# Layer 2 of a two-layer image network: LayerNorm with tokens on partitions, the depthwise convolution inside the input projection, and a written plan for the order of the work

## The chip, the cores and the metric

The kernel runs on one core of a Trainium2 chip, in float32. The metric is the device time of one execution in microseconds. Engines are named as in the profile: PE multiplies matrices and transposes, DVE is the vector engine, ACT computes functions of one argument with a scale and a bias for each partition, POOL is the fourth one, SP issues DMAs.

## The reference, cut to what matters

Four images of 192 channels and 128 x 128 pixels go through two residual layers. The first (spectral, FFT and fractional FFT) is not touched. The second is a selective state-space layer over the 16,384 pixels of an image taken as a sequence of tokens, on the group-normalised image:

```python
x = x + layer1(group_norm(x))          # layer1, for tokens l and channels c:
seq = (seq - mu) * rsqrt(var + 1e-5) * ln_g + ln_b        # over the 192 channels of a token
xs, z = split(in_proj_w @ seq)                            # 384 and 384
u  = silu(depthwise_conv(xs, 4 taps, causal) + conv_b)
dt, B, C = split(x_proj_w @ u)                            # 12, 16, 16
dt = softplus(dt_proj_w @ dt + dt_proj_b)
for each token l:                                         # state h: 384 x 16
    h = h * exp(dt[l] * A) + (dt[l] * u[l]) * B[l]
    y[l] = sum over states of h * C[l]
out = out_proj_w @ ((y + u * D) * silu(z))
```

## The kernel before

`layer0` runs first and leaves its result in DRAM (`xmid`) and the group norm's mean and scale for each channel in `st2`. `layer1` then takes the four images one after the other in chunks of T = 512 tokens: 32 chunks an image, 128 in all. The 384 inner channels are three tiles j of 128 partitions, the 16 states are eight pairs sg. A chunk is therefore 24 steps (`NGR`), step k being tile k // 8 and pair k % 8, and the kernel 3072 steps. `order` lists them, and the loop over `order` writes the instructions of every engine in one hand-made order (the scheduler is off).

**A step.** DVE runs two scans of 512 tokens, one for each state of the pair, into `h` (L903); each takes a decay exp(dt A) from ACT (L833) and an input dt u B. POOL multiplies both states by C (L916, `hc`). Three steps later (LAG) PE adds the pair into `py` with eight transposing passes (L929, `sums`). The last value of each scan goes to the next chunk by a small DMA (L914).

**Where the input dt u B comes from** depends on the pair. V pairs: DVE multiplies the PSUM copy `dp` of dt u (L816, ACT) by B (L853, `product`), two states ahead, into one of three PSUM tiles `op`. O pairs (BY_POOL, 7 a chunk): POOL makes both states at once (L861, `inputs`), and the decay goes to an `op` tile instead. P pairs (BY_PE, pairs 3 and 6 of each tile, 6 a chunk): dt u is turned to tokens by PE (L867, `turned`), ACT scales it by B there, four blocks a state (L877, `scale_pair`), and PE turns it back into an `op` tile (L889, `turned_back`). That leaves 11 V pairs.

**After the eight pairs of a tile** come `add_skip` (L943, u D on PE), `evacuate` (L938, ACT copies `py`), `turn` (L953, PE turns it to channels) and `gate` (L958, DVE multiplies by silu(z)). After three tiles, `finish` projects out in two halves (L967, PE) and DVE adds the residual (L973).

**The front** makes dt, u, z, B and C for a chunk two ahead. It is the generator `front`, advanced by one `yield` a step; a plain yield goes on at the start of the next step, MID between the two scans of it, LATE after them. With channels on partitions it normalises (L643), sums over channels by PE (L650), subtracts (L653, DVE), squares (L658), sums again (L666), takes root and reciprocal (L673, L676), and brings the result for each token back to all channels by a transpose and four small matmuls (L678, L682, L686) for DVE's second pass (L691). Then come the input projection (L697), the copy of its x half with three columns of the chunk before (L706, L710, L711), the convolution as four diagonal matmuls a tile (L716), silu (L724, L728), the projection to dt, B, C (L762, L765) with a trip through DRAM for B and C (L767), dt (L776, contraction over 12 rows; L781), dt u (L785, POOL), B by tokens (L791, L794) and the other two z tiles.

B and C are read back for a pair of states at a time, broadcast to 128 partitions, 1 MB a DMA (L807, `load_bc`), into eight buffers, five steps ahead.

**What sets the order.** Each engine runs its instructions in the order written; SP's queue holds load_bc, the carries, the loads and stores. An instruction that waits for a buffer holds all behind it. PSUM has eight banks: three that everything of `psum()` takes in turn (`ps1`), one for `dp`, three for `op`, one for `py`.

Of the kernel before, what the change touches and what calls it, by code (L numbers as in the profile page):

```python
# [10 lines left out]
F32 = mybir.dt.float32  # L11
# [3 lines left out]
ALU = mybir.AluOpType  # L15
# [518 lines left out]

def layer1(tc, xmid, out, st2, w, n_tok=S * S):
# [5 lines left out]
    LAG, FRONT, BCL = 3, 14, 5  # L541
    AHEAD = 4

    BY_POOL = ((1, 4, 7), (1, 7), (1, 7))
    BY_PE = 3, 6
    MID, LATE = "mid", "late"

    TURNED = {0: 0, 9: 1, 15: 2, 19: 2}
    SCALED = {0: (0, 3), 3: (0, 6), 9: (1, 3), 11: (1, 6), 16: (2, 3), 20: (2, 6)}
    with ExitStack() as ctx:  # L550
# [5 lines left out]
        xp = pool("l1x", 3)  # L556
# [3 lines left out]
        bcp = pool("l1b", NS // G)  # L560
        scp = pool("l1s", 4)
        op = pool("l1o", 1)
        ps1 = pool("l1p", 3, space=PSUM)
        psd = pool("l1q", 1, space=PSUM)
        psa = pool("l1a", 3, space=PSUM)
        psy = pool("l1y", 1, space=PSUM)

        def const(name):
            src = w[name]
            t = cp.tile(list(src.shape), F32, name="c_" + name)  # L570
            nc.sync.dma_start(out=t, in_=src)
            return t

        wiT, ln_g, ln_b, xpT, dtT, dtb = (const(k) for k in ("wiT", "ln_g", "ln_b", "xpT", "dtT", "dtb"))
        cw, cb, dp, woT, A = (const(k) for k in ("cw", "cb", "dp", "woT", "A_log"))

        ident = cp.tile([128, 128], F32, name="ident")
        make_identity(nc, ident)
        ones = cp.tile([128, CH], F32, name="ones")
        nc.vector.memset(ones, 1.0)  # L580
        sel = cp.tile([4, 4, CH], F32, name="sel")
        nc.vector.tensor_copy(sel, _bc(ident[0:4, 0:4], 2, CH))
# [7 lines left out]
        )  # L590


        bxz = cp.tile([128, 2 * NJ], F32, name="bxz")
        ps = ps1.tile([128, 512], F32, name="ps")
        for m in range(2 * NJ):
            for t in range(2):
                nc.tensor.matmul(
                    ps[:, m : m + 1], wiT[:, t, m * 128 : (m + 1) * 128], ln_b[:, t : t + 1],
                    start=t == 0, stop=t == 1,
                )  # L600
        nc.vector.tensor_copy(bxz, ps[:, 0 : 2 * NJ])
        for t in range(2):
            nc.vector.tensor_scalar(wiT[:, t, :], wiT[:, t, :], ln_g[:, t : t + 1], None, ALU.mult)

# [6 lines left out]
        dcw = cp.tile([128, NJ, 4, 128], F32, name="dcw")  # L611
        for j in range(NJ):
            for k in range(4):
                nc.vector.tensor_scalar(dcw[:, j, k, :], ident, cw[:, j, k : k + 1], None, ALU.mult)

        halo = cp.tile([128, NJ, 3], F32, name="halo")
        last = {}

        def psum():
            return ps1.tile([128, 512], F32, name="ps")  # L620

# [4 lines left out]

        def load_x(i):
            b, ch = divmod(i, NCHUNK)
            xm = xp.tile([CH, 2, T], F32, name="xm")
            nc.sync.dma_start(  # L630
                out=xm, in_=xmid[b][:, ch * T : (ch + 1) * T].rearrange("(t p) f -> p t f", p=CH)
            )
            got[i]["xm"] = xm

        def front(i):

            b, ch = divmod(i, NCHUNK)
            g = got[i]
            xm = g["xm"]
            yield MID  # L640
            s = lp.tile([CH, 2, T], F32, name="s", bufs=2)
            for t in range(2):
                nc.scalar.activation(  # L643
                    s[:, t, :], xm[:, t, :], AF.Identity,
                    bias=nmr[:, b, t : t + 1], scale=st2[:, b, t, 1:2],
                )
            yield
            mu = psum()
            for t in range(2):
                nc.tensor.matmul(mu[0:CH], ones[0:CH, :], s[:, t, :], start=t == 0, stop=t == 1)  # L650
            yield
            yield MID
            nc.vector.scalar_tensor_tensor(  # L653
                s, _bc(mu[0:CH], 1, 2), -1.0 / C, s, ALU.mult, ALU.add
            )
            yield
            sq = lp.tile([128, NJ, T + 3], F32, name="xs")[0:CH, 0:2, 0:T]
            nc.scalar.activation(sq, s, AF.Square)  # L658
            yield


            yield LATE
            var = psum()
            for q in range(4):
                for t in range(2):
                    nc.tensor.matmul(  # L666
                        var[:, q : q + 1], sq[:, t, q * 128 : (q + 1) * 128], ones[0:CH, 0:1],
                        start=t == 0, stop=t == 1,
                    )
            yield  # L670
            yield LATE
            rs = tp.tile([128, 4], F32, name="rs")
            nc.scalar.activation(rs, var[:, 0:4], AF.Sqrt, bias=eps, scale=1.0 / C)  # L673
            yield
            yield LATE
            nc.vector.reciprocal(rs, rs)  # L676
            rt = psum()
            nc.tensor.transpose(rt[0:4, 0:128], rs, ident)  # L678
            yield
            yield MID  # L680
            rows = tp.tile([4, 128], F32, name="rows")
            nc.scalar.copy(rows, rt[0:4, 0:128])  # L682
            yield LATE
            rb = psum()
            for q in range(4):
                nc.tensor.matmul(  # L686
                    rb[0:CH, q * 128 : (q + 1) * 128], sel[:, q, :], rows, start=True, stop=True
                )
            yield
            yield MID  # L690
            nc.vector.tensor_tensor(s, s, _bc(rb[0:CH], 1, 2), ALU.mult)  # L691
            yield

            def in_proj(m):
                pp = psum()
                for t in range(2):
                    nc.tensor.matmul(  # L697
                        pp, wiT[:, t, m * 128 : (m + 1) * 128], s[:, t, :], start=t == 0, stop=t == 1
                    )
                return pp  # L700

            xs = lp.tile([128, NJ, T + 3], F32, name="xs")
            if ch == 0:
                nc.gpsimd.memset(xs[:, :, 0:3], 0.0)
            else:
                nc.scalar.copy(xs[:, :, 0:3], halo)  # L706
            for j in range(NJ):
                pp = in_proj(j)
                yield
                nc.scalar.activation(xs[:, j, 3:], pp, AF.Identity, bias=bxz[:, j : j + 1])  # L710
            nc.scalar.copy(halo, xs[:, :, T : T + 3])  # L711
            yield LATE

            def conv(j, pc, half):
                for k in (2 * half, 2 * half + 1):
                    nc.tensor.matmul(  # L716
                        pc, dcw[:, j, k, :], xs[:, j, k : k + T], start=k == 0, stop=k == 3
                    )

            u, zs = g["u"], g["zs"] = {}, {}  # L720

            def silu_u(j, pc):
                u[j] = jp.tile([128, T], F32, name="u")
# [506 lines left out]
```

## Time and profile before

| | us |
|---|---|
| median of three runs | 11368.98 |
| lowest and highest of them | 11358.7, 11369.3 |
| profiled execution, span | 11364.2 |
| first scan of layer1 (L903) | 1426.8 |
| last scan of layer1 ends | 11347.4 |
| a chunk, from 77.5 = (11347.4 - 1426.8) / 128 | 77.5 |

The profile is of one execution; its span lies 4.8 us under the median of the runs. A line of groups has the line in the code, engine, operation, output <- inputs, partitions x elements, how many, then busy time in us and the mean of one in ns, then the idle time of the engine just before such instructions and what ended it. "PEld" is PE's weight load, which overlaps its matmuls. A matmul of float32 counts as two instructions. In the table of windows, a number in brackets is a count, and the granted clock of PE is 1.00 at full speed. "bc" and "ps" are names that several tiles share.

### The profile page before, as it was taken

What the parts mean: (1) busy time and instruction counts of PE and PEld (TensorE: products, weight loads), DVE (VectorE), ACT (ScalarE), POOL (GpSimd) and SP (SyncE); (2) the same over time, 40 slices, a digit from 0 to 9 for tenths busy, and PEclk for the clock granted to TensorE, in tenths of its full rate; (3) what the DMA queues carried; (4) which work ended last, traced back from release to release, by engine and by line L of the source; (5) the groups of instructions that cost most, each with busy time, mean ns of one, the idle gap of its engine ahead of it and who ended that gap; (6) DMA issues with size and microseconds to landing.
All of it is one profiled execution on the core that took longest, in us unless ns stands there. A gap on an engine that the chain in (4) does not pass through costs nothing.

```text
span 11364.2 us, 163771 instructions
## 1 busy us (share of the span) xinstructions
PE 10431.7 (92%) x54154; PEld 6995.9 (62%) x54154; DVE 10480.6 (92%) x11073; ACT 9340.5 (82%) x17503; POOL 9811.8 (86%) x4470
## 2 busy tenths in 40 slices
PE   4777799999999999999999999999999999999998
PEld 2444366666666666666666666666666666666666
DVE  5666599999999999999999999999999999999999
ACT  2332189989989989999989989989989999899897
POOL 0000099999999999999999999999999999999999
PEclk8888699999999999999999999999999999999998
DMA  8786644344344344344344344344344344344343
GB/s 233 195 219 170 199 123 129 108 126 129 107 126 129 107 126 129 106 127 129 105 128 129 105 128 129 104 128 129 104 128 129 104 129 129 103 129 128 104 130 99
DMA packets 1339287, 1481.93 MB, mean 130 GB/s; under 512 B 903281, under 2 KB 954214, under 8 KB 1337926
## 3 DMA queue, kind: packets, MB, share of 16 engines
q1 hardware_dynamic: 1317958, 1408.54, 42.2%
q0 software_dynamic: 13312, 50.34, 1.4%
q10 hardware_dynamic: 7168, 12.59, 0.3%
q8 instruction: 429, 7.03, 0.2%
q14 instruction: 420, 3.44, 0.1%
HBM read 1312.63 MB, written 155.32 MB: 129 GB/s over the span
## 4 chain that ended last, share of the span: by engine, by line
ACT 28%; DVE 27%; PE 25%; issue 8%; POOL 3%; DMA 1%; DVEq 0%; POOLq 0%; SPq 0%; ACTq 0%
DVE h L903 18%; ACT da L833 8%; DVE op L853 6%; PE py L929 6%; ACT dbT L877 6%; PE ps L697 4%; PE ps L716 4%; PE ps L967 4%; ACT L833 3%; PE op L889 2%; POOL db L861 2%; ACT op L833 1%; ACT L724 1%; ACT dt L781 1%; PE ps L686 1%
## 5 line engine op out<-in xcount | busy, mean ns | idle before, releaser
L916 POOL TENSOR_TENSOR hc<-h,bc 128x1024 f32<-128x1024 f32 x3072 | 7203.0, 2381 | 217.6 <-PE ps L953 145.8
L903 DVE TENSOR_TENSOR_SCAN h<-da,carry,op 128x512 f32<-128x512 f32 x4216 | 5198.7, 1261 | 22.6 <-ACT da L833 6.1
L929 PEld LDWEIGHTS py<-ident,hc 128*128 128x128 f32 x24576 | 3002.6, 149 | 855.2 <-issue 698.4
L929 PE MATMUL py<-ident,hc 128*128 128x128 f32 x24576 | 3406.0, 286 | 32.6 <-ACT yt L938 19.1
L833 ACT ACTIVATE da<-dt,c_A_log 128x512 f32<-128x512 f32 x4352 | 3003.7, 727 | 181.9 <-DVE h L903 161.6
L903 DVE TENSOR_TENSOR_SCAN h<-op,carry,db 128x512 f32<-128x512 f32 x1736 | 2200.7, 1268 | 124.2 <-POOL db L861 119.6
L861 POOL TENSOR_TENSOR db<-dtu,bc 128x1024 f32<-128x1024 f32 x896 | 2152.9, 2403 | 4.5 <-DMA bc<-dbc 4.5
L853 DVE TENSOR_TENSOR op<-dp,bc 128x512 f32<-128x512 f32 x2816 | 1886.0, 670 | 11.2 <-ACT dp L816 11.2
L833 ACT ACTIVATE op<-dt,c_A_log 128x512 f32<-128x512 f32 x1792 | 1227.0, 685 | 674.1 <-DVE h L903 671.0
L877 ACT ACTIVATE dbT<-ps,bT 128x128 f32<-128x128 f32 x6144 | 1666.6, 383 | 0.0
L697 PE MATMUL ps<-s,c_wiT 96*128 96x512 f32 x3072 | 1529.3, 622 | 5.2 <-ACT xs L710 3.6
L716 PE MATMUL ps<-xs,dcw 128*128 128x512 f32 x3072 | 1426.6, 593 | 1.4 <-ACT u L724 1.4
L889 PE MATMUL op<-ident,dbT 128*128 128x128 f32 x6144 | 1075.3, 295 | 102.1 <-DVE h L903 71.7
L889 PEld LDWEIGHTS op<-ident,dbT 128*128 128x128 f32 x6144 | 779.8, 151 | 397.2 <-ACT dbT L877 204.8
L697 PEld LDWEIGHTS ps<-s,c_wiT 96*128 96x128 f32 x3072 | 559.2, 199 | 473.7 <-issue 463.6
L833 ACT ACT_TABLE_LOAD x635 | 814.7, 1283 | 11.2
L716 PEld LDWEIGHTS ps<-xs,dcw 128*128 128x128 f32 x3072 | 533.9, 190 | 434.9 <-issue 433.3
L967 PE MATMUL ps<-yg,c_woT 128*96 128x512 f32 x1536 | 710.5, 598 | 70.3 <-DVE xm L973 70.2
L776 PE MATMUL ps<-xd,c_dtT 12*128 12x512 f32 x768 | 512.6, 756 | 162.2 <-DVE s L653 94.8
L495 POOL DMA_DIRECT2D xmid<-xt x64 | 41.7, 652 | 567.7 <-DVE xt L491 523.0
L967 PEld LDWEIGHTS ps<-yg,c_woT 128*96 128x96 f32 x1536 | 239.9, 163 | 436.9 <-issue 321.6
L785 POOL TENSOR_TENSOR dtu<-dt,u 128x512 f32<-128x512 f32 x384 | 479.3, 1284 | 33.8 <-ACT dt L781 33.8
(172 smaller groups left out, 10196.2 us busy)
## 6 DMA issues: line engine op xcount, KB each, us to landing
bc<-dbc SPq DMA_DIRECT2D x1024, 1024.0 KB, 5.7
xt<-in_x SPq DMA_DIRECT2D x176, 768.0 KB, 8.1
xmid<-xt POOLq DMA_DIRECT2D x64, 768.0 KB, 5.6
xm<-xmid SPq DMA_DIRECT2D x128, 384.0 KB, 3.5
carry<-h SPq DMA_DIRECT2D x3072, 1.0 KB, 1.9
out<-xm SPq DMA_DIRECT2D x128, 384.0 KB, 3.3
d<-x ACTq DMA_DIRECT2D x64, 192.0 KB, 6.6
df<-v SPq DMA_DIRECT2D x16, 512.0 KB, 5.4
```

The source lines that it names most:

```text
L697: nc.tensor.matmul(pp, wiT[:, t, m * 128 : (m + 1) * 128], s[:, t, :], start=t == 0, stop=t == 1)
L716: nc.tensor.matmul(pc, dcw[:, j, k, :], xs[:, j, k : k + T], start=k == 0, stop=k == 3)
L776: nc.tensor.matmul(d[j], dtT[rows, :], xd[rows, :], start=True, stop=True)
L833: nc.scalar.activation(da, got[n]["dt"][j], AF.Exp, scale=A[:, j, st : st + 1])
L853: nc.vector.tensor_tensor(dbs[s], g["dp"], g["bc", k % NG][:, 0, q, :], ALU.mult)
L861: nc.gpsimd.tensor_tensor(db, _bc(g["dtu"][j], 1, G), g["bc", sg][:, 0], ALU.mult)
L877: nc.scalar.activation(t[:, blk, :], g["tu", j][:, blk, :], AF.Identity, scale=g["bT"][:, blk, st : st + 1],)
L889: nc.tensor.transpose(db[:, blk * 128 : (blk + 1) * 128], t[:, blk, :], ident)
L903: nc.vector.tensor_tensor_scan(h[:, q, :], das.pop(s), dbs.pop(s) if db is None else db[:, q, :], 0.0 if ch == 0 else g["before"][:, j, st ...
L916: nc.gpsimd.tensor_tensor(hc, h, g["bc", sg][:, 1], ALU.mult)
L929: nc.tensor.matmul(py[:, blk, :], hc[:, q, blk * 128 : (blk + 1) * 128], ident, start=first, stop=sg == NG - 1 and q == G - 1 and blk == T ...
L967: nc.tensor.matmul(po[0:CH], woT[:, j, t * CH : (t + 1) * CH], g["yg", j], start=j == 0, stop=j == NJ - 1,)
```

## The change

It rewrites `layer1`; `layer0` stays. In the words of the code:

- LayerNorm. `to_tokens` multiplies the loaded x by a diagonal matrix `gd` of the group norm's scales, with a row of its shifts under a row of ones, so that tokens come out on partitions, two blocks of 128 tokens a bank. `moments` takes bn_stats and bn_aggr over the 192 channels on DVE, `rstd` is Ln and Exp on ACT, `shift` a small DVE instruction, `normed` four activations; `to_channels` turns the result back, and `channels` applies ln_g and ln_b on ACT and keeps three columns of the chunk before in `s`.
- The convolution is applied in the input projection. The weights `wc` are products of taps and projection, made once at the start. A tile takes six matmuls of 128 rows: four taps of the first 128 channels, and two that hold two taps of the other 64 channels each, for which a DMA copies `s[0:64]` to `s[64:128]` shifted by two columns.
- A third P pair in each tile: KINDS gives the kind of each pair, now 9 P, 6 O and 9 V. `dbT` has four buffers instead of two.
- PSUM: five banks in one list, taken by `psum` in the order of use and given back by `done`, and the three of `op` as before.
- B and C are loaded by DMAs of their own, 512 KB each; B of pair 3, which is P in all tiles, is not loaded.
- The order: PLAN says for each piece of a chunk's work the step, counted from the chunk's first, and the place in the step: S at its start, A after `turned_back` and `sums`, M between the two scans, L at its end. `log_exp` loads the table with ln and exp after each group of silu or softplus.

Cut to its core:

```diff
+KINDS = ("VOPPVVPO", "VOVPOVPP", "VOVPVPPO")
+PLAN = (
+    (-36, "A", "load_x"), (-34, "L", "to_tokens", 0), (-32, "S", "moments", 0),
+    (-32, "A", "to_tokens", 1), (-31, "S", "moments", 1), (-31, "A", "rstd"), (-30, "S", "shift"),
+    (-30, "M", "normed", 0), (-30, "M", "normed", 1), (-29, "S", "to_channels", 0),
+    (-29, "A", "channels", 0), (-28, "M", "to_channels", 1), (-28, "M", "channels", 1),
+    (-27, "S", "conv", 0, 0), (-27, "L", "conv", 1, 0), (-26, "L", "conv", 1, 1),
+    (-25, "M", "conv", 0, 1), (-24, "M", "conv", 1, 2), (-22, "L", "conv", 2, 0),
+    (-21, "M", "conv", 0, 2), (-21, "L", "silu", (0, 1), ()), (-17, "S", "conv", 2, 1),
+    (-16, "A", "conv", 2, 2), (-15, "L", "proj_z", 0), (-15, "L", "silu", (2,), (0,)),
+    (-13, "M", "proj_x"), (-11, "S", "xd_out"), (-11, "M", "proj_dt"), (-10, "M", "softplus"),
+    (-9, "M", "turn_b"), (-8, "A", "b_out"), (-7, "A", "dt_u", 0), (-7, "A", "dt_u", 1),
+    (-3, "L", "turned", 0), (-3, "L", "scale", 0, 2), (-2, "S", "dtu_copy", 0),
+    (1, "S", "dt_u", 2), (1, "A", "scale", 0, 3), (2, "S", "scale", 0, 6),
+    (4, "M", "dtu_copy", 1), (6, "S", "turned", 1), (6, "A", "scale", 1, 3),
+    (10, "S", "scale", 1, 6), (10, "A", "scale", 1, 7), (10, "M", "evacuate", 0),
+    (10, "M", "proj_z", 2), (11, "A", "proj_z", 1), (11, "M", "silu", (), (1, 2)),
+    (11, "L", "turn", 0), (12, "L", "dtu_copy", 2), (13, "M", "gate", 0), (16, "L", "turned", 2),
+    (17, "S", "scale", 2, 3), (17, "L", "scale", 2, 5), (19, "S", "scale", 2, 6),
+    (19, "M", "evacuate", 1), (21, "A", "turn", 1), (22, "S", "gate", 1),
+    (26, "L", "evacuate", 2), (29, "A", "turn", 2), (30, "A", "gate", 2),
+    (31, "A", "project_out", 0), (32, "L", "add_x", 0), (34, "S", "project_out", 1),
+    (35, "M", "add_x", 1),
+)
...
+        banks = list(range(5))
+        def psum(g, *key):
+            bank = banks.pop(0)
+            g[key] = ps1.tile([128, 512], F32, name=f"ps{bank}"), bank
+        def done(g, *key):
+            banks.append(g.pop(key)[1])
...
+            for blk in (2 * half, 2 * half + 1):
                 for t in range(2):
                     nc.tensor.matmul(
-                        var[:, q : q + 1], sq[:, t, q * 128 : (q + 1) * 128], ones[0:CH, 0:1],
+                        row(g, blk)[:, t * CH : (t + 1) * CH],
+                        g["xm"][:, t, blk * 128 : (blk + 1) * 128], gd[:, i // NCHUNK, t, :],
+                        start=True, stop=True,
+                    )
...
+            for blk in range(2):
+                nc.vector.bn_stats(st[:, blk, :], row(g, 2 * half + blk))
+            for blk in range(2):
+                nc.vector.bn_aggr(g["mv"][:, 2 * half + blk, :], st[:, blk, :])
...
+            nc.scalar.activation(rs, g["mv"][:, :, 1], AF.Ln, bias=eps)
+            nc.scalar.activation(rs, rs, AF.Exp, scale=-0.5)
...
+            for k in (2 * part, 2 * part + 1):
+                rhs = s[:, 0, k : k + T] if k < 4 else s[:, 1, 3 - 2 * (k - 4) :][:, 0:T]
+                nc.tensor.matmul(g["c", j][0], wc[:, j, k, :], rhs, start=k == 0, stop=k == 5)
...
+            if part == 1:
+                nc.sync.dma_start(out=s[64:128, 1, 1 : T + 3], in_=s[0:64, 1, 0 : T + 2])
...
+            for j in us:
+                t = g["u", j] = jp.tile([128, T], F32, name="u", bufs=5)
+                nc.scalar.activation(t, g["c", j][0], AF.Silu, bias=cb[:, j : j + 1])
+                done(g, "c", j)
+            for j in zs:
+                t = g["zs", j] = jp.tile([128, T], F32, name="zs", bufs=5)
+                nc.scalar.activation(t, g["z", j][0], AF.Silu)
+                done(g, "z", j)
+            log_exp()
...
             for pos, (n, k) in enumerate(order):
                 j, sg = divmod(k, NG)
+                act(pos, "S")
+                turned_back(G * (pos + 1))
                 if pos >= LAG and sg != LAG:
                     sums(*order[pos - LAG])
+                act(pos, "A")
                 if pos + 2 < len(order):
                     inputs(*order[pos + 2])
+                scans(pos, n, k, lambda: act(pos, "M"))
+                act(pos, "L")
                 if pos >= LAG and sg == LAG:
                     sums(*order[pos - LAG])
                     add_skip(n, j)
```

In a chunk's steps, with three chunks in work at a time, PE then meets in one step what PLAN gives for this chunk and for those one and two ahead: at step 10 project_out 1 of the chunk before and z2 of its own, at step 13 gate 0 and d of the next (-11), and so on.

## The prediction

> **What bounds the kernel now.** I read the page's first part, then the stretch from 5700 to 7700 us as windows and as groups, then single rows of the timeline, and last the waits.
>
> ```profile
> span 11364.2 us, 163771 instructions
> PE 10431.7 (92%) x54154; PEld 6995.9 (62%) x54154; DVE 10480.6 (92%) x11073; ACT 9340.5 (82%) x17503; POOL 9811.8 (86%) x4470
> ```
>
> This mixes layer 0, in which POOL does next to nothing, with 10,000 us of chunks. In a steady stretch it is closer:
>
> ```profile
> 6055.10:6061.90 6.80, 6.80 (x20) 3.92 (x19) 6.80 (x8) 6.75 (x14) 6.80 (x4) 0.50 0.04 0
> 5986.00:5989.40 3.40, 3.02 (x28) 2.81 (x28) 3.40 (x5) 3.38 (x7) 3.40 (x3) 1.00 0.12 26
> 5700.00:7700.00 2000.00, 1908.89 (x10255) 1304.06 (x10253) 1939.94 (x2015) 1810.82 (x3431) 1957.89 (x880) 0.95 0.40 119
> ```
>
> The columns after the length are PE, PEld, DVE, ACT, POOL, granted clock, DMA share, GB/s.
>
> ```profile
> L916 POOL TENSOR_TENSOR hc<-h,bc 128x1024 f32<-128x1024 f32 x620 | 1452.0, 2373 | 42.1 <-PE ps L953 29.9 <-DVE h L903 11.9
> L861 POOL TENSOR_TENSOR db<-dtu,bc 128x1024 f32<-128x1024 f32 x181 | 433.7, 2396 | 0.0
> L877 ACT ACTIVATE dbT<-ps,bT 128x128 f32<-128x128 f32 x1240 | 336.4, 383 | 0.0
> L833 ACT ACT_TABLE_LOAD x129 | 165.5, 1283 | 2.3
> L653 DVE SCALAR_TENSOR_TENSOR s<-ps,s 96x1024 f32<-96x1024 f32 x26 | 31.0, 1193 | 0.0
> L691 DVE TENSOR_TENSOR s<-s,ps 96x1024 f32<-96x1024 f32 x25 | 30.4, 1217 | 28.0 <-PE ps L686 28.0
> ```
>
> 620 hc at 24 a chunk are 25.83 chunks in 2000 us: **77.4 us a chunk**. In it POOL is busy 1957.89/25.83 = 75.8 us, DVE 75.1, PE 73.9, ACT 70.1. No engine has 8 us to spare, so the pace comes from two full engines that wait for each other, and through short queues also for PE. POOL's own idle is 1.6 us a chunk, most of it hc waiting for L953's turn on PE; DVE's 2.3 is half L691's wait for PE.
>
> A row's mean is longer than what an instruction costs in a row of its kind, since the next starts before the last ends. Start to start comes from the timeline:
>
> ```profile
> 6000.35 0.67 DVE L853 TENSOR_TENSOR op<-dp,bc 128x512 f32<-128x512 f32 x1
> 6000.93 1.27 DVE L903 TENSOR_TENSOR_SCAN h<-op,carry,db 128x512 f32<-128x512 f32 x1
> 6001.08 1.04 PE L929 MATMUL py<-ident,hc 128*128 128x128 f32 x8
> 6001.95 1.88 PE L697 MATMUL ps<-s,c_wiT 96*128 96x512 f32 x4
> 6002.71 2.44 DVE L903 TENSOR_TENSOR_SCAN h<-da,carry,op 128x512 f32<-128x512 f32 x2
> 6003.67 1.04 PE L929 MATMUL py<-ident,hc 128*128 128x128 f32 x8
> 6004.23 7.01 POOL L916 TENSOR_TENSOR hc<-h,bc 128x1024 f32<-128x1024 f32 x3
> 6007.03 2.16 ACT L877 ACTIVATE dbT<-ps,bT 128x128 f32<-128x128 f32 x8
> ```
>
> and, a chunk earlier, PE alone:
>
> ```profile
> 5978.96 1.12 PE L776 MATMUL ps<-xd,c_dtT 12*128 12x512 f32 x2 [0.59 <-ACT dbT L877]
> 5980.01 1.97 PE L929 MATMUL py<-ident,hc 128*128 128x128 f32 x8
> ```
>
> So a product takes 0.58 us (0.93 less 0.35), a scan 2.44 - 1.26 = 1.18, eight 128-column passes 0.87 (0.109 each), four 512-column passes 1.72 (0.43 each; a float32 matmul is two passes), hc (7.01 - 2.37)/2 = 2.32, a dbT (2.16 - 0.38)/7 = 0.25, a pass of d (L776) 1.05/2 = 0.53. At 5980.01 eight passes take 1.97 where they took 1.04: PE is at half clock there, as in the window from 6055.1, behind another d.
>
> **What the Trainium skill says.** "TensorE: Matmul & The Clock Gate", "Part 1: The HAM clock gate": an activity window of about 3.4 us decides between full and half clock. The trace agrees: stretches at 0.50 are 3.4 or 6.8 us long and follow d, whose operands have 12 rows. Its Part 4 says that transposes don't count as activity; the window from 5986, nearly all transposes, is at 1.00, which speaks against it, if weakly. The same page, "Architectural detail": PE pulls only weight loads ahead, ACT and DVE are strictly first in, first out. So a matmul that waits for its bank holds everything behind it; L776's waits in the middle of d above are such. "ScalarE: Activation LUTs", "Table sets": one set holds exp and ln, so the new Ln + Exp needs no load beside the decays' exp; no row of before shows it. No page read for this prices bn_stats.
>
> **The change, part by part**, per chunk, against 77.4 us.
>
> *POOL*: O pairs 7 to 6, one db less: 75.8 - 2.34 = 73.4.
>
> *DVE*: V pairs 11 to 9, four products less, -2.33. L653, L691 and the reciprocal go, -2.34. Two moments (four bn_stats of 192 elements and four bn_aggr) and the shift come. Layer 0's bn_stats of 512 takes 0.68; 192 of it between 0.25 and 0.4, a tiny instruction 0.15 to 0.19: bounds 1.6 to 2.4 with the shift, I take 1.95. Sum 75.1 - 4.67 + 1.95 = 72.4.
>
> *ACT*: P pairs 6 to 9 are 24 dbT, +6.1. Gone: two s, Square, Sqrt, rows, three xs and a halo copy, 1.6 + 1.1 + 0.3 + 0.25 + 2.15 + 0.2 = 5.6 by row means, and two of ten table loads, 2.6. New: Ln and Exp 0.5, four normed of 192 columns (bounds 0.3, 0.45) 1.4, two channels 1.3. Sum 70.1 + 1.1 = 71.2.
>
> *PE*: gone are mu 1.7, var 1.8, rb and rt 1.0, in_proj's x half 12 passes 5.2, the convolution's 24 passes 10.3, one turned 0.4: 20.4. New: 36 passes of the joint convolution 15.5, to_tokens 1.8, to_channels 0.9, back transposes 2.6: 20.8. Load +0.4, nothing; order is what matters.
>
> *SP and DMA*: load_bc becomes 15 issues of 512 KB for 8 of 1 MB, with shift's copy 43 issues for 35. At some 0.6 us each (an estimate: 25 us in 77) SP still idles, and the DMA share is 0.40, so I cost them at nothing; with the first taps on the copied rows four steps after it, that cover is some 10 us. If it were gone, conv's third part would hold PE for a DMA's 2 us.
>
> *Prologue*: the dnmr round trip, gd and 2 MB of broadcast taps, +5 us once (bounds -5, +15). First scan 1426.8 before, the end 16.8 after the last scan.
>
> By loads alone POOL would pace at 73.4. **Waits decide otherwise.** Five banks in one list now tie instructions of different kinds: po1 (step 10) takes the bank that silu of u2 frees. That silu stands on ACT behind the decays that wait for the last scan of step 8, and behind a table load. Behind po1 stands PE's whole queue. From the end of that scan: decay 0.62, load 1.30, silu 0.69; then PE in its written order up to the transposes that the scan of step 15 reads: po1 six passes 2.58, five back transpositions (11, 11, 14, 14, 15) 2.2, sums of steps 7 to 10 3.5, z2 and z1 3.44, px 2.58, turn 0.44, add_skip 0.9, d 3.2: 18.8. With 0.35 for four handovers 21.8 us. DVE's own work there, steps 9 to 14, is 12 scans 14.2, four products 2.3, two add_x and a gate 1.75: 18.3. **DVE stalls 3.45 us at step 15**; POOL, fed by DVE's scans, stalls with it, and no buffer holds more than a step or two to carry it over.
>
> A second, smaller burst: from the first scan of step 20, back transpositions of 21 and 22 0.87, to_channels 0.44, four conv passes 1.72, sums 0.87, turn 0.44 and handovers 0.3 bring gate 1 to 5.9 us after step 20's start where DVE would be there at 4.75: 1.15.
>
> DVE 72.4 + 3.45 + 1.15 = 77.0. Half clock after d: one window costs PE up to 1.7 us (half of 3.4); part falls on the chain, part into PE's slack of steps 16 to 18. Bounds 0 and 1.7, I take 0.7. L686's window and its waits for DVE and POOL are gone, and are replaced by these. **77.7 us a chunk.**
>
> Sum: 1426.8 + 5 + 128 x 77.7 + 16.8 = 11394 against the execution's own 11364.2; the median of the runs is 4.8 above its span, so 11399, say 11400 us.
>
> **Rivals.** (a) *Faster, the bursts are absorbed.* If PE comes to po1 with its bank free, or has worked ahead by the 3.45 us, DVE never sees the burst. The point from which it decides: silu of u2 done when PE has finished step 9. For it: no single engine is over 73.4, PE could start all of it earlier. Against: ACT's decays wait for scans (29.4 us of waits in the groups), so silu cannot run ahead. Then POOL's 73.4 and the idle that it has now, 1.7: 75.1, 1453.4 + 128 x 75.1 = 11066. (b) *Slower, more half clock.* d now lies right behind px, turns and sums, and with the long in_proj and conv matmuls moved, stretches from step 14 to 18 hold only transposes and to_tokens. A second window on every chunk, inside the path, costs its 1.7: 79.5, 11630. (c) *It moves nothing.* PE, whose load stays, may already set the pace through the buffers, with 73.9 busy and 3.5 idle; then what is taken from DVE and POOL only makes them wait: 77.4 and the prologue, 11364.2 + 5 + 4.8 = 11374 (11350 to 11390). For it: PE is busy 95% of the stretch. Against: DVE waits for PE only 1.1 us a chunk now, at L691.
>
> **Chances.** What a measurement here can tell from no change is about 0.2%, 23 us: faster is under 11346, slower over 11392. Forecast 0.52, own range 11310 to 11510 (half clock 0 to 1.7, moments' bounds): 0.10 of it faster, 0.08 same, 0.34 slower. (a) 0.28, faster. (b) 0.10, slower. (c) 0.10, same. Together 0.38, 0.18, 0.44. For the range, the lowest quarter of (a) and most of (b) are left out, 0.16: 11040 to 11560.
>
> **What would show it.** Right: DVE idle of 4 to 5 us a chunk, half or more of it scans that wait for PE's back transpositions (L889 now) at steps 14 to 16; PE waiting for ACT u at po1; POOL idle of about 4 us; no wait of DVE for a broadcast of rstd; eight table loads a chunk; half clock behind d only. Wrong: POOL busy over 97% with chunks of 75 us (then (a)); a granted clock under 0.93 in the same stretch (then (b)); waits for shift's copy or load_bc on PE or POOL; Ln with loads of its own.

## The result, and the profile after

The changed kernel takes 11266.8 us (median of four runs, 11264.5 to 11273.8) against 11366.5 for the kernel before in the same comparison: a ratio of 0.9915, 95% interval 0.9901 to 0.9929. It is faster where a little slower was forecast, 133 us under the forecast and inside its wide range. Its profiled execution spans 11262.4 us.

The same stretch as before, as a window (PE, PEld, DVE, ACT, POOL, clock, DMA share, GB/s):

```profile
5700.00:7700.00 2000.00, 1853.05 (x10768) 1306.32 (x10763) 1898.57 (x2090) 1874.67 (x4011) 1921.77 (x863) 0.98 0.37 110
```

and its groups that answer to those shown of before:

```profile
L951 POOL TENSOR_TENSOR hc<-h,c 128x1024 f32<-128x1024 f32 x627 | 1474.0, 2377 | 78.8 <-DVE h L938 72.5 <-PE op L924 4.4 <-PE ps L723 0.9
L892 POOL TENSOR_TENSOR db<-dtu,b 128x1024 f32<-128x1024 f32 x157 | 377.1, 2402 | 0.0
L909 ACT ACTIVATE dbT<-ps,bT 128x128 f32<-128x128 f32 x1872 | 502.8, 402 | 13.2 <-PE ps L901 12.9
L996 DVE TENSOR_TENSOR yg<-ps,zs 128x512 f32<-128x512 f32 x78 | 52.5, 673 | 32.2 <-PE ps L989 32.2
L693 DVE BATCH_NORM_STATS2 st<-ps 128x6 f32<-128x192 f32 x106 | 32.4, 347 | 0.0
L706 DVE SCALAR_TENSOR_TENSOR sh<-mv,rs 128x4 f32<-128x4 f32 x26 | 20.5, 788 | 0.0
```

627 hc are 26.1 chunks: 76.6 us each instead of 77.4 (77.7 forecast). A chunk now has POOL busy for 73.6 us, DVE 72.7, ACT 71.8, PE 70.9. DVE is idle 3.9 us a chunk, 1.24 of it at gate 1 (32.2 us over 26 chunks). Two rows are odd: a shift of four columns (L706) takes 788 ns, more than twice what bn_stats of 192 columns takes; and d does not appear among the long ones. Where it runs, PE's timeline of one chunk shows this:

```profile
5837.30 0.24 PEld L1003 LDWEIGHTS ps<-yg,c_woT 128*96 128x96 f32 x2 [0.88 <-ACT u L767]
...
5841.70 1.02 PE L760 MATMUL ps<-s,wz 128*128 128x512 f32 x2
...
5845.81 2.84 PE L779 MATMUL ps<-u,c_xpT 128*128 128x512 f32 x6
...
5853.41 1.13 PE L795 MATMUL ps<-xd,c_dtT 12*128 12x512 f32 x6
5854.48 0.66 PE L924 MATMUL op<-ident,dbT 128*128 128x128 f32 x4
```

project_out 1 (L1003) waits for silu of u2 as forecast. z2 and z1, between 5841.70 and 5845.81, take 4.1 us. But the six passes of d (L795), six times 0.53 in the forecast, are over in 5854.48 - 5853.41 = 1.07 us. DVE in the same chunk, and one decay on ACT:

```profile
5844.30 0.82 ACT L860 ACTIVATE op<-dt,c_A_log 128x512 f32<-128x512 f32 x1
...
5845.20 1.28 DVE L938 TENSOR_TENSOR_SCAN h<-op,carry,db 128x512 f32<-128x512 f32 x1 [1.35 <-issue]
...
5852.38 2.49 DVE L938 TENSOR_TENSOR_SCAN h<-da,carry,op 128x512 f32<-128x512 f32 x2 [0.58 <-ACT xd L784]
...
5855.34 1.28 DVE L938 TENSOR_TENSOR_SCAN h<-da,carry,op 128x512 f32<-128x512 f32 x1 [0.47 <-PE op L924]
```

The scans are those of steps 12, 14 and 15. "Issue" is time for which the view shows no releaser; ACT's decay of step 12 was late there: it ends at 5845.12, and the scan begins at 5845.20. The stall of the first burst is there, 2.4 us in this chunk and 2.2 on average, but only its last 0.47 stands at step 15.

### The profile page after: what moved, and what is told of

Read it like the earlier page. It is cut to its first block, busy times and chain, and to the rows that moved or that the text cites. A ratio compares the mean times of both kernels' runs of the same rounds, so it can differ in the third digit from the quotient of the medians.

```text
span 11262.4 us, 172048 instructions
## 1 busy us (share of the span) xinstructions
PE 10025.0 (89%) x56050; PEld 6906.9 (61%) x56050; DVE 10180.0 (90%) x11329; ACT 9562.4 (85%) x20200; POOL 9530.1 (85%) x4342
## 5 line engine op out<-in xcount | busy, mean ns | idle before, releaser
L951 POOL TENSOR_TENSOR hc<-h,c 128x1024 f32<-128x1024 f32 x3072 | 7220.3, 2377 | 400.6 <-DVE h L938 371.5
L964 PE MATMUL ps<-ident,hc 128*128 128x128 f32 x24576 | 3278.8, 278 | 10.8 <-POOL hc L951 10.8
L964 PEld LDWEIGHTS ps<-ident,hc 128*128 128x128 f32 x24576 | 2892.2, 144 | 485.1 <-issue 458.5
L909 ACT ACTIVATE dbT<-ps,bT 128x128 f32<-128x128 f32 x9216 | 2475.7, 402 | 76.4 <-PE ps L901 65.3
L754 PE MATMUL ps<-s,wc 128*128 128x512 f32 x4608 | 2162.5, 596 | 23.7 <-DMA s<-s 7.6
L892 POOL TENSOR_TENSOR db<-dtu,b 128x1024 f32<-128x1024 f32 x768 | 1843.9, 2401 | 5.0 <-DMA b<-dbc 5.0
L881 DVE TENSOR_TENSOR op<-ps,b 128x512 f32<-128x512 f32 x2304 | 1548.5, 672 | 9.4 <-ACT ps L842 9.4
L754 PEld LDWEIGHTS ps<-s,wc 128*128 128x128 f32 x4608 | 795.4, 190 | 673.2 <-issue 628.5
L1003 PE MATMUL ps<-yg,c_woT 128*96 128x512 f32 x1536 | 710.5, 598 | 7.6 <-ACT u L767 0.3
L1003 PEld LDWEIGHTS ps<-yg,c_woT 128*96 128x96 f32 x1536 | 233.1, 163 | 384.9 <-issue 273.0
L761 PE MATMUL ps<-s,wz 64*128 64x512 f32 x768 | 431.0, 641 | 0.0
L760 PE MATMUL ps<-s,wz 128*128 128x512 f32 x768 | 419.3, 628 | 0.7 <-DVE xm L1010 0.5
```

The source lines that it names most:

```text
L754: nc.tensor.matmul(g["c", j][0], wc[:, j, k, :], rhs, start=k == 0, stop=k == 5)
L881: nc.vector.tensor_tensor(dbs[s], g["dp", j][0], g["b", k % NG][:, q, :], ALU.mult)
L892: nc.gpsimd.tensor_tensor(db, _bc(g["dtu", j], 1, G), g["b", sg], ALU.mult)
L909: nc.scalar.activation(t[:, blk, :], g["tu", j][0][:, blk * 128 : (blk + 1) * 128], AF.Identity, scale=g["bT"][:, blk, st : st + 1],)
L951: nc.gpsimd.tensor_tensor(hc, h, g["c", "b", sg], ALU.mult)
L964: nc.tensor.matmul(py[:, blk, :], hc[:, q, blk * 128 : (blk + 1) * 128], ident, start=first, stop=sg == NG - 1 and q == G - 1 and blk == N ...
```

## The experiments

All are edits of the changed kernel but for one, which edits the kernel before. Times are medians; a ratio is to the kernel before, run beside it, with its 95% interval. From one group of runs to another the kernel before itself took 11360 to 11371 us, so between groups a difference of some 10 us, 0.1 us a chunk, says nothing.

**d on one row group**

```diff
+        dt0 = cp.tile([RANK, NJ, 128], F32, name="dt0")
+        for j in range(NJ):
+            nc.sync.dma_start(out=dt0[:, j, :], in_=w["dtT"][32 * j : 32 * j + RANK, :])
...
-                rows = slice(32 * j, 32 * j + RANK)
-                nc.tensor.matmul(g["d", j][0], dtT[rows, :], g["xd"][rows, :], start=True, stop=True)
+                nc.tensor.matmul(g["d", j][0], dt0[:, j, :], g["xd"][0:RANK, :], start=True, stop=True)
```

> The six passes of d all use rows 0 to 11 of the array and of xd (the same numbers), so they can't run side by side; nothing else differs from the changed kernel (11267 us, 76.7 us a chunk). If PE's burst still ends last at step 15, as its 0.46 us wait there says, d grows from 1.06 to 3.2 us, the wait at step 15 by nearly 2.1, and the time to about 11267 + 128 x 2.1 = 11535. That would give back the size that the prediction put on the burst. If ACT's queue alone sets steps 12 to 15 and PE only looks late, PE has room for it: 11270 to 11330.

11502.5 us, ratio 1.0119 (1.0104 to 1.0134): slower than before the change. In its timelines, PE's and DVE's in the same chunk,

```profile
5801.59 2.84 PE L797 MATMUL ps<-xd,dt 12*128 12x512 f32 x6
5804.36 0.66 PE L926 MATMUL op<-ident,dbT 128*128 128x128 f32 x4
```

```profile
5800.55 2.49 DVE L940 TENSOR_TENSOR_SCAN h<-da,carry,op 128x512 f32<-128x512 f32 x2 [0.58 <-ACT xd L787]
5805.22 1.28 DVE L940 TENSOR_TENSOR_SCAN h<-da,carry,op 128x512 f32<-128x512 f32 x1 [2.17 <-ACT dt L803]
```

d takes 2.77 us, 1.70 more, and the wait at step 15 grows from 0.47 to 2.17, by the same 1.70. (The view names ACT's softplus as releaser; it lies behind d too, and PE's back transposition for this scan comes directly after d.) The time grows by (11502.5 - 11266.8) / 128 = 1.84 us a chunk. Some 0.15 of this goes with half clock, which begins at steps 14 and 15 in 40 of the 128 chunks here; those chunks take 0.5 us longer than the others. So in the changed kernel the tiles of d, whose operands lie on rows 0, 32 and 64, run side by side, and each microsecond of d counts in full. The Trainium skill has it: "TensorE: Matmul & The Clock Gate", "Part 3: Packing small matmuls — row/col tiling", says that matmuls on different rows of the array overlap, starting some 4 ns apart; the three start 7 ns apart in the trace.

**d over all 128 rows**

```diff
+        dt0 = cp.tile([128, NJ, 128], F32, name="dt0")
+        nc.vector.memset(dt0, 0.0)
+        for j in range(NJ):
+            nc.sync.dma_start(out=dt0[32 * j : 32 * j + RANK, j, :], in_=w["dtT"][32 * j : 32 * j + RANK, :])
...
-                nc.tensor.matmul(g["d", j][0], dtT[rows, :], g["xd"][rows, :], start=True, stop=True)
+                nc.tensor.matmul(g["d", j][0], dt0[:, j, :], g["xd"], start=True, stop=True)
```

> d contracts over all 128 rows with zero weights on those of the other tiles: six passes that can't run side by side, of 0.43 us, 2.6 in all instead of 3.2 in the run on one row group and 1.06 in the changed kernel. Passes over 128 rows are followed by no half clock so far, so this tells what the half clock is worth: against the run on one row group (11502) the 0.6 us that d is shorter give 11425; if the half clock behind d was on the path there, as the prediction has it with 0.7 us a chunk, 11335. The granted clock of the stretch should go from 0.96 to 1.00 in both cases.

11435.6 us (1.0044 to 1.0071 of before): d takes 2.58 us, 1.51 more than in the changed kernel, and the time is 1.32 us a chunk longer, so d's length counts here too. What half clock is worth the run doesn't tell, since half clock didn't go: it begins at step 17 or 18 in 127 of the 128 chunks (89 in the changed kernel), though d has all its rows. One such window, and PE about its start:

```profile
5864.30:5871.10 6.80, 4.92 (x23) 4.91 (x24) 6.80 (x8) 6.77 (x24) 6.56 (x5) 0.50 0.04 0
```

```profile
5860.86 1.04 PE L967 MATMUL ps<-ident,hc 128*128 128x128 f32 x8
5866.18 1.09 PE L927 MATMUL op<-ident,dbT 128*128 128x128 f32 x4 [4.29 <-DVE h L941]
```

PE had run ahead and waited 4.3 us for DVE's scans. In the changed kernel's trace half clock goes with such waits, not with d. The clock goes down and up at multiples of 3.41 us. Cut there, all 90 stretches of layer 1 at full clock after which it falls have PE busy for at most 0.41 of the time, and all 2601 after which it stays have PE busy for 0.42 or more (an instruction counted to its end or to the next one's start). 55 of the latter hold nothing but transposes, for over 0.9 of the time, so transposes kept the clock up, as the prediction suspected. (Its own window from 5986 shows that less well: 8 of the 28 matmuls there belong to `add_skip`.) Half clock follows d itself only where d is long: with PE busy all the time in the run on one row group, and in the kernel before, where 187 of the 190 stretches before half clock hold d or the broadcast L686, matmuls of 12 and 4 rows.

In the window PE is busy 4.92 of 6.80 us even at half speed, and DVE is busy for all of it and waits for nothing. In the changed kernel a chunk takes 76.6 us without half clock (34 chunks), 76.7 with 3.41 us of it (59) and 77.1 with 6.8 us (25; the first and last of each image left out): on average 0.1 us a chunk.

**Less ACT in step 11** (silu of z1 and z2 left out)

```diff
-                nc.scalar.activation(t, g["z", j][0], AF.Silu)
+                nc.scalar.activation(t, g["z", j][0], AF.Silu if us else AF.Copy)
-            log_exp()
+            if us:
+                log_exp()
```

> z1 and z2 are copied without their silu (that silu is left out), which saves two table loads a chunk, 2.6 us of ACT in step 11, and nothing on PE. If ACT's queue is what ends last in steps 12 to 14 (DVE's waits for it there are 1.0 us a chunk with the one put to issue), 11267 - 128 x 1.0 = 11140. If PE's burst ends last, its px, d and back transposition come as late as now and the waits move to step 15: 11240 to 11270.

11267.3 us: 2.6 us of ACT in the burst bring nothing. The waits at steps 12 to 15 stay 2.1 us, partly under other names. This leaves out ACT's work alone; see the run with project_out 1 moved and a V pair, below.

**shift with one operand in PSUM**

```diff
+            nc.scalar.activation(lv, g["mv"][:, :, 1], AF.Ln, bias=eps)
+            nc.scalar.activation(g["X", 1][0][:, 2 * C : 2 * C + NBLK], lv, AF.Exp, scale=-0.5)
             nc.scalar.activation(rs, lv, AF.Exp, scale=-0.5)
...
+            rs = g["X", 1][0][:, 2 * C : 2 * C + NBLK]
             nc.vector.scalar_tensor_tensor(sh, g["mv"][:, :, 0], -1.0, rs, ALU.mult, ALU.mult)
```

> rstd is also written to unused columns of the PSUM bank of to_tokens, and shift reads it there, so this DVE instruction has one operand in SBUF instead of two. In the changed kernel it takes 0.77 us and ends 0.02 us after the POOL instruction that runs when it starts, and in the run with two P pairs 4.1 us, behind two of them. If it waits there for POOL, it falls to about 0.16 and DVE gains 0.6 us a chunk, ACT pays 0.2: 11267 - 78 = 11190 if DVE's work is on the path there, 11250 to 11270 if gate 1's wait takes it. If the time comes from the instruction itself, it stays at 0.77 and so does the time.

11198.1 us, ratio 0.9850 (0.9837 to 0.9864): 0.54 us a chunk gained. The group is now

```profile
L709 DVE SCALAR_TENSOR_TENSOR sh<-mv,ps 128x4 f32<-128x4 f32 x26 | 3.9, 151 | 0.0
```

The instruction is the same but for where one operand lies. What it waited for is plainest in the run with two P pairs, below, on POOL and then on DVE:

```profile
6160.03 2.54 POOL L808 TENSOR_TENSOR dtu<-dt,u 128x512 f32<-128x512 f32 x2
6162.48 2.39 POOL L951 TENSOR_TENSOR hc<-h,c 128x1024 f32<-128x1024 f32 x1
```

```profile
6160.81 4.08 DVE L706 SCALAR_TENSOR_TENSOR sh<-mv,rs 128x4 f32<-128x4 f32 x1
6164.82 1.27 DVE L938 TENSOR_TENSOR_SCAN h<-da,carry,op 128x512 f32<-128x512 f32 x1
```

It starts beside POOL's work and ends at 6164.89, 0.02 us after hc. With both operands in SBUF too, but at the start of the changed kernel where POOL does nothing beside it, shift takes 0.16:

```profile
1414.36 0.16 DVE L706 SCALAR_TENSOR_TENSOR sh<-mv,rs 128x4 f32<-128x4 f32 x1 [0.71 <-ACT rs L701]
```

The Trainium skill, "SBUF — State Buffer", "Who interferes with whom", states that a DVE instruction with two inputs in SBUF contends with a POOL instruction that reads SBUF, and that the later one blocks until the other ends. The trace agrees that shift waits, and shows the waiting time as busy time, so no list of waits names it. It doesn't wait for one instruction only, though: at 6160.81 the first of the two dtu is under way, and the second dtu and hc, which begin later, both pass before shift.

**Two P pairs again**, without and with that mend

```diff
-KINDS = ("VOPPVVPO", "VOVPOVPP", "VOVPVPPO")
+KINDS = ("VOVPOVPO", "VOVPVVPO", "VOVPVVPO")
...
-    (-3, "L", "scale", 0, 2),
...
-    (10, "A", "scale", 1, 7),
...
-    (17, "L", "scale", 2, 5),
```

> The kinds of the pairs as before the change (7 O, 6 P, 11 V), all else as in the changed kernel. DVE +2.3 us a chunk (four products), POOL +2.3 (one db), ACT -6, PE -2.6. If DVE's work plus its waits make the period: DVE 75.2, POOL 75.8, and waits that shrink from 3.9 to 2 since ACT's burst at step 10 loses eight dbT: 77.2 to 77.7 a chunk, 11335 to 11400, that is no faster than the kernel before; then the third pair is the whole gain. If ACT paces the changed kernel, which loses 6 us here: 76 or less, under 11180.

> The kinds of before and shift with its second operand in PSUM. If the 4.1 us of shift were what made the run with two P pairs slow, 81.9 - 3.9 = 78.0 to 78.6 a chunk: 11440 to 11510, and the third pair is worth 1.5 to 2 us a chunk. If that time only covers a wait that comes anyway (for POOL's three db of the first tile, 2.3 us at step 4), 81 and more: 11800.

11925.3 us (1.0469 to 1.0504) and 11484.7 us (1.0091 to 1.0119). The 4.1 us of shift made 3.4 us a chunk of the first: 440 us for one small instruction that meets POOL at another moment. The two kernels with the mend, with two pairs and with three, differ by (11484.7 - 11198.1) / 128 = 2.2 us a chunk: that is the third pair's worth in this plan. All the rest of the change, with two pairs and shift mended, is 1% slower than the kernel before, with DVE waiting 2.1 us a chunk for POOL's db at step 4 of tile 0, the pair that needs no db with three P pairs. A plan made for these kinds might do better; that wasn't tried.

**Gate 1 and the work around it**: gate 1 later; the convolution behind turn 1; and the convolution there with turned and its dbT behind the dp copy (this last with shift mended)

```diff
-    (-2, "S", "dtu_copy", 0),
+    (-2, "M", "dtu_copy", 0),
...
-    (22, "S", "gate", 1),
+    (22, "M", "gate", 1),
...
-    (-27, "S", "conv", 0, 0)
+    (-27, "A", "conv", 0, 0)
...
-    (-3, "L", "turned", 0), (-3, "L", "scale", 0, 2), (-2, "S", "dtu_copy", 0)
+    (-2, "S", "dtu_copy", 0), (-2, "L", "turned", 0), (-2, "L", "scale", 0, 2)
```

> gate 1 moves from the start of step 22 to between its scans, and the dp copy of the next chunk's first tile behind it. DVE waits 1.24 us a chunk for PE's turn at gate 1. If that wait lies on the path, up to 1.2 us a chunk go: 11267 - 150 = 11115. If PE and ACT, not DVE, set the end of that stretch, the wait turns up at the next product or scan: 11250 to 11280; if the later dp copy delays the products of the next chunk, slower, up to 11350.

> At step 21 the first part of the convolution (four passes, 1.72 us of PE) comes after turn 1 instead of ahead of it. Gate 1's wait for that turn, 1.24 us a chunk, goes. If it was on the path, the second burst of the prediction, 11267 - 128 x 1.2 = 11110; if PE, 1.7 us later with its convolution, then holds the back transpositions of step 23 and on, the wait moves there: 11250 to 11290.

> Shift's operand in PSUM, the convolution of step 21 after turn 1, and the first turned and its eight dbT half a step behind the dp copy instead of ahead of it. In the run with the convolution alone the wait at gate 1 went and came back as products that wait for the dp copy (0.4 to 0.6 us), which stands on ACT behind those dbT, and they behind PE. If that is the second link of the same wait, both now go: 11198 - 100 = 11100 or lower. If something else of the same length stands behind it (decays, back transpositions at step 26), 11180 to 11210.

11295.0, 11279.1 and 11204.8 us, against 11266.8, 11266.8 and 11198.1: the wait at gate 1 goes each time, and nothing is gained. In the second,

```profile
5891.87 2.18 ACT L909 ACTIVATE dbT<-ps,bT 128x128 f32<-128x128 f32 x8 [0.80 <-PE ps L901]
5893.89 0.65 ACT L842 COPY ps<-dtu 128x512 f32<-128x512 f32 x1
5894.57 0.70 DVE L881 TENSOR_TENSOR op<-ps,b 128x512 f32<-128x512 f32 x1 [0.61 <-ACT ps L842]
```

the dp copy stands behind eight dbT that wait for PE. In the third that is mended too, and DVE waits at step 1 for the carry DMA (0.5 us a chunk) and dbT (0.4).

**A pair of POOL's to DVE**, at step 12, at step 12 with the convolution moved, at step 1 (shift mended)

```diff
-KINDS = ("VOPPVVPO", "VOVPOVPP", "VOVPVPPO")
+KINDS = ("VOPPVVPO", "VOVPVVPP", "VOVPVPPO")
...
+KINDS = ("VVPPVVPO", "VOVPOVPP", "VOVPVPPO")
```

> The kernel with shift's operand in PSUM (11198 us, 76.15 a chunk), and the pair of step 12 (tile 1, pair 4) made V instead of O: POOL loses a db of 2.34 us, DVE gets two products, 1.17. POOL works without a gap from step 20 to step 12 of the next chunk, and DVE waits 1.16 us at step 12. If POOL paces that stretch and PE the burst from 12 to 15, the wait at step 12 goes and the products lie in DVE's waits at steps 14 and 15: 75.0 or a little less, 11050. If DVE's own work sets the pace (72.2 of 76.15), 1.17 more of it gives 11350; if PE alone does, 11198.

> The same with the convolution of step 21 after turn 1. Behind a POOL that is full, gate 1's wait could not be won back (11279 against 11267). If POOL was the reason and step 12's V pair takes 2.34 us from it, the 1.1 us at gate 1 now count: 11050 - 130 = 10920. If not, like the run without it.

> As the V pair of step 12, but at step 1 (tile 0, pair 1): the same work moved from POOL to DVE at another place, where DVE has no wait of size. If POOL's stretch from 20 to 12 is what counts, 1.17 of DVE against 2.34 of POOL gives a gain of the same kind, 11050 to 11130; if what helped was that the products fall into DVE's waits at 12 to 15, DVE's stretch grows by 1.17: 11198 to 11340.

11215.1, 11228.3 and 11308.5 us against 11198.1. At step 12 DVE's 1.17 us cost 0.13: they lie in its waits, and the 2.34 taken from POOL bring nothing. At step 1 they cost 0.86: outside the burst DVE's work counts nearly in full. That POOL alone paces is refuted.

**project_out 1 out of the burst**, with add_x 1 ahead of step 16's scans, the same with gate 1's moves, add_x 1 between the scans, that with step 12's V pair, and all together (shift mended; x in two tiles, more buffers)

```diff
-    (34, "S", "project_out", 1), (35, "M", "add_x", 1),
+    (39, "L", "project_out", 1), (40, "S", "add_x", 1),
...
+    (39, "L", "project_out", 1), (40, "M", "add_x", 1),
```

> Shift's operand in PSUM, and project_out 1 (2.58 us of PE) moved from step 10 to the end of step 15, behind the burst, with add_x 1 at step 16 (x in two tiles, four buffers for the second half, four yg, zs by tile). If PE's burst is what makes DVE wait at steps 12 to 15 (2.2 us with the issue part), as d's length showed, those waits shrink to under 0.5 and the time by 1.5 to 2 us a chunk: 10950 to 11010. If PE's load there only hides ACT's or POOL's, the waits keep to steps 12 and 14: 11130 to 11200.

> Both moves together. If the two bursts are separate links of one chain through DVE, the gains add up: the sum of the two others' gains against 11198, so 10850 to 10910. If they share slack (POOL's 73.5 us becomes the limit), no better than 73.5 + 1.5 = 75 a chunk, 11050.

> As the run with project_out 1 at the end of step 15, but add_x 1 between the scans of step 16, not ahead of them, where DVE waited 2.4 us for PE. That wait goes and what the move does for steps 12 to 15 is seen: there the waits fell from 2.2 (0.6 at step 14 gone) to 2.3 with more of it for POOL's db at step 12. If PE's burst was the limit, 11198 less 0.5 to 1 us a chunk: 11070 to 11140. If POOL and ACT stand directly behind it, 11180 to 11220; if add_x still waits for PE, over 11250.

> The same with the pair of step 12 made V. If PE's burst and POOL's db at step 12 are two limits of nearly the same length, each of which hides the other (a V pair alone gave 11215, project_out alone is the run beside this), both moves together show what neither does: 75.2 a chunk or less, under 11090. If a third (ACT's decays, the wait put to issue at step 13) is as long, 11180 to 11220.

> Also the convolution of step 21 behind turn 1, and turned and its dbT behind the dp copy. With POOL relieved of a db and PE of its burst, the wait at gate 1 (1.1 to 1.3 us) should count at last: 1.0 us a chunk below the run with two moves. If it still counts for nothing, a limit that none of these moves touches stands there.

11485.3, 11484.1, 11250.4, 11253.0 and 11254.6 us, against 11198.1. The first two were placed badly: add_x waits 2.3 us for PE at step 16. Between the scans it still waits 0.3 there, and PE's 2.6 us out of the burst gain nothing (0.4 us a chunk are lost): the wait at step 14 is gone, but that at step 12 is 1.7 us instead of 1.2 in the kernel with only shift mended (1.2 of it named POOL's db). With a V pair there too, that one goes as well and 1.4 us come at step 13, put to issue. There ACT is late:

```profile
5839.19 1.28 ACT L774 ACT_TABLE_LOAD   x1
5840.48 1.08 ACT L774 ACTIVATE zs<-ps 128x512 f32<-128x512 f32 x2
5841.59 1.28 ACT L661 ACT_TABLE_LOAD   x1
5842.88 2.56 ACT L863 ACTIVATE da<-dt,c_A_log 128x512 f32<-128x512 f32 x4
```

```profile
5843.69 1.28 DVE L941 TENSOR_TENSOR_SCAN h<-da,carry,op 128x512 f32<-128x512 f32 x1 [1.31 <-issue]
```

The decay for this scan stands behind silu of z1 and z2 and its two table loads, and in 25 of 26 chunks it ends less than 0.13 us before the scan. So behind the waits for PE and POOL comes a third, for the very work that the run without silu left out alone. All three taken away together were not tried, so it isn't shown that they do no more than hide each other, nor that they do.

**The kernel before, d a step later**

```diff
+            yield
+            yield LATE
             d = [psum() for _ in range(NJ)]
...
             z1 = in_proj(NJ + 1)
             yield
-            yield
```

> The kernel before, with d one step later (and z2 a step sooner behind z1, so that the rest of the front keeps its length). In its trace the three tiles' d are 1.9 and 1.7 us apart, each waiting for its bank, and take 4.7 us of PE. If the banks are free a step later and the passes run side by side, the six take 1.1 us. DVE waits for PE there only at L691, so the time moves little, 11300 to 11370; if passes on other rows don't run side by side in this kernel, d takes 3.2 us.

11495.3 us, ratio 1.0108 (1.0094 to 1.0121), a miss twice over: d takes as long as before, and L691's wait grows from 1.1 to 2.4 us a chunk.

```profile
6025.79 2.19 PE L777 MATMUL ps<-xd,c_dtT 12*128 12x512 f32 x4
6028.55 2.03 PE L777 MATMUL ps<-xd,c_dtT 12*128 12x512 f32 x2 [0.58 <-ACT dbT L877]
```

```profile
6025.60 1.20 DVE L653 SCALAR_TENSOR_TENSOR s<-ps,s 96x1024 f32<-96x1024 f32 x1
```

The first two tiles follow without a gap and take 0.53 us a pass, as if they could not run side by side. But the second tile, which starts at 6026.85, waits for a bank that DVE's L653 gives back at 6026.80. In 126 of the 128 chunks it starts 0.055 us after L653's end, and in the seven of these in which L653 ends sooner it starts while the first tile runs. In the last chunk no L653 stands before it, and it starts 7 ns after the first tile:

```profile
11364.81 1.13 PE L777 MATMUL ps<-xd,c_dtT 12*128 12x512 f32 x4
```

So the passes run side by side in this kernel as well, as soon as they have their banks. Why L691 waits longer was not looked into.

## Why the prediction was wrong, step by step

**Loads: right.** POOL 73.4 forecast, 73.6 measured; DVE 72.4 and 72.7; ACT 71.2 and 71.8; eight table loads a chunk, none for Ln. PE was to stay at 74.3 and fell to 70.9, the first sign of d, whose row was 4.0 us a chunk before and is 1.2 now. Two halves of DVE's sum were off and cancel in part: moments cost 1.5 instead of 1.8 us, shift 0.77 instead of 0.15. The prediction priced shift by its size alone, not by where its operands lie.

**SP, DMA and prologue: right.** POOL waits for a load of C 0.03 us a chunk. The first scan comes 1.7 us sooner, but the first chunk takes 82.9 us, 6.1 more than the later ones (1.0 more in the kernel before): 3.4 us once, 5 forecast.

**The first burst: right in its mechanism, wrong in one term.** "d 3.2" is the step that failed. It was read off before's rows, where each tile of d waits for its own bank, so that they come one after the other; nothing there said that they must. The last chunk of before's trace says the opposite, for there the second tile's bank is free:

```profile
11169.74 1.12 PE L776 MATMUL ps<-xd,c_dtT 12*128 12x512 f32 x2
11171.64 1.12 PE L776 MATMUL ps<-xd,c_dtT 12*128 12x512 f32 x2 [0.78 <-DVE s L653]
...
11245.71 1.13 PE L776 MATMUL ps<-xd,c_dtT 12*128 12x512 f32 x4
```

Two tiles take there what one takes elsewhere. In the changed kernel d is 1.07. From the end of step 8's scans (5834.43) to step 15's scan it is 20.9 us instead of 21.8, not 19.7, for other terms of the same sum were too small: z2 and z1 take 4.1 instead of 3.44, and the handovers, project_out 1 and px some 0.5 more. So the stall is 2.2 us a chunk where 1.3 would be left of 3.45 with d alone put right. It stands at steps 12, 14 and 15 (1.1, 0.6 and 0.5), not at 15 alone: at step 12 DVE waits for decays and POOL's db, of which the prediction said nothing.

**The second burst: right in size, not in worth.** Gate 1 waits 1.24 us, 1.15 forecast. Three runs took the wait away and gained nothing.

**Half clock: 0.7 forecast, some 0.1 measured.** It doesn't follow d. It comes at steps 17 and 18, where rival (b) had feared a second window, because PE waits there, and so it finds PE with room.

**The sum** as measured: DVE busy 72.7, 2.2 at steps 12 to 15, 1.2 at gate 1 and 0.4 of smaller waits are 76.5, against 76.6 by the count of hc; the forecast had 72.4, 3.45, 1.15 and 0.7. The d term was 2.1 us too long and half clock 0.6, together more than twice the miss of about 1 us; terms that were too small or not in the sum made up for the rest. That the number came so near was luck in this: with d on one row group, still shorter than forecast, the kernel is slower than before, and 100 us slower than the forecast.

**The rivals.** (a) did not come: the bursts hold, at 76.6, not 75.1. (b) and (c) did not either. The kernel came out faster for a reason that stands in none of them. In which place the next limit lies stays open. At steps 12 to 15 waits for PE, POOL and ACT take each other's place when one or two of them are moved, and no such move gained anything; d's length, shift's lock, the third pair and DVE's own work outside the burst did change the time. At gate 1, what follows is seen (the dp copy, then the carry DMA at step 1), but a run that takes all of these away was not found.

The fastest version is the changed kernel with shift's operand in PSUM: 11198.1 us, 0.9850 of the kernel before (0.9837 to 0.9864).

## What to carry to other kernels

A duration read from a row holds with that row's waits: ask whether the instruction was alone by need or because of a bank, before it is multiplied, and look for one instance without the wait. Price small instructions by where their operands lie as well as by their size. And a wait that is seen, even forecast to a tenth, is worth only what stands behind it: test it by moving it before it goes into a sum.

## What was not expected of the hardware

- Three tiles of d on rows 0, 32 and 64 take 1.07 us for six float32 passes of 512 columns; on one row group 2.77, over 128 rows 2.58. Where a tile's bank comes late, it starts 0.055 us after the bank is free, beside the tile that runs.
- A DVE instruction of 128 x 4 with both operands in SBUF takes 0.16 us with POOL idle, 0.77 beside POOL, up to 4.1 where POOL's next instructions get ahead of it, and 0.15 with one operand in PSUM. The profile counts the wait as busy.
- In the changed kernel half clock followed stretches of 3.41 us in which PE was busy for 0.41 or less, and never one with 0.42 or more. Transposes counted as busy; passes of 12 and 4 rows, in the kernel before, did not keep the clock up.
